# Expert rows loaded as 32-wide squares and transposed by VectorE instead of TensorE

## The chip, the cores and the metric

The kernel runs on one core of a Trainium2 chip. The metric is the device time of one execution in microseconds, the median of several runs.

## The reference, cut to what matters

One layer with attention and a mixture of experts side by side, in fp32. Input `x` has 16 batches of 512 tokens with 128 features; there are 8 experts of hidden width 512, and each token goes to its best two.

```python
xn = layernorm(x)
attn = causal_attention(l2norm(xn @ Wq), l2norm(xn @ Wk), xn @ Wv, scale=8) @ Wo   # 16 heads of 8
probs = softmax(xn @ Wr.T)
top_v, top_i = top_k(probs, 2); top_v = top_v / top_v.sum()
for e in range(8):
    w_e = where(top_i == e, top_v, 0).sum(-1)
    moe += (gelu(xn @ W1[e].T + b1[e]) @ W2[e].T + b2[e]) * w_e
out = x + attn + moe
```

## The kernel before, in words

The first part of the kernel normalises the tokens, routes them and works through the attention of 14 of the 16 batches. Along the way GpSimd sends each normalised token, with its routing data, into a table `slots` in DRAM, sorted by expert: 128 indirect DMAs (`send`). A row of `slots` has 132 floats: 128 features and then the token's place, its first expert, its gate and the difference to the second gate.

The expert stage (`experts`) follows. It takes `slots` in 71 blocks of 256 rows, where a block belongs to one expert. For block i it does the following.

- `fetch(i)` runs on SyncE's queue. It reads the block's expert from `bexp_i`, then issues the loads: the block's rows `xg` (L783), the expert's two weight matrices `w1` (L786) and `w2` (L787), each 256 KB, and the output bias `bb` (L790). The weights go into six buffers that held the transposed tokens `xnT` before, so the profile calls them xnT.
- `turn_rows(i)` makes `xgT`, features on the partitions and 256 tokens along the row: two TensorE transposes into PSUM (L796), a VectorE copy (L798), and three small VectorE instructions for the targets and gates (L801, L807, L811).
- `hidden(i)` multiplies by `w1` (L817), and ScalarE applies gelu (L820) into `gT`.
- `mix(i)` multiplies by `w2` into the one PSUM bank `av` (L828). VectorE adds the bias (L833) and multiplies by the gate (L836), and GpSimd scatters the rows of `y` into the table `results` (the L502 helper).

The order on TensorE, SyncE, VectorE and ScalarE is written out by hand and kept. In step i of the loop stand `hidden(i)`, `turn_rows(i + 1)`, `mix(i - 1)` and at its end `fetch(i + 5)`. The first five fetches come ahead of the loop, and the first of all waits until the last `send` has landed. Each of SyncE's DMAs also waits until the DMA eight places ahead of it on that queue has landed, because eight semaphores go round.

After the blocks come the attention of the last two batches, the loads of `results` (`bring`), the sums into `x` (L908) and the stores.

Of the kernel before, what the change touches and what calls it, by code (L numbers as in the profile page):

```python
# [10 lines left out]
F32 = mybir.dt.float32  # L11
I32 = mybir.dt.int32
AF = mybir.ActivationFunctionType
ALU = mybir.AluOpType
# [10 lines left out]
def attention_moe_kernel(  # L25
# [19 lines left out]
    nc = tc.nc  # L45
    B, S, D = x.shape
    E = wrT.shape[1]
    M = w1T.shape[2]
    P = 128
# [4 lines left out]
    TB = 32  # L54
# [10 lines left out]
    BT = 2 * P  # L65
# [4 lines left out]
    ROW = D + 4  # L70
# [33 lines left out]
    slots = dram.tile([SLOTS, ROW], F32, name="slots")  # L104
# [3 lines left out]
    ident = const.tile([P, P], F32, name="ident")  # L108
# [43 lines left out]
    bexp = keep.tile([P, NB], F32, name="bexp")  # L152
# [18 lines left out]
    def misc(name):  # L171
        return ps_m.tile([P, 512], F32, tag="misc", name=name)
# [49 lines left out]
    def scales(b0, b1, root):  # L222

        cols = slice(b0 * NC, b1 * NC)
        n = (b1 - b0) * NC
        have = {}

        even, odd = st[:, cols, 1], st[:, cols, 4]

        def variance():  # L230
            dif = have["dif"] = sm.tile([P, n], F32, tag="dif", name=f"dif{b0}")
            var = have["var"] = sm.tile([P, n], F32, tag="var", name=f"var{b0}")
            nc.vector.tensor_sub(dif, even, odd)
            nc.vector.tensor_mul(var, dif, dif)
            nc.vector.scalar_tensor_tensor(
                var, var, D / 4.0, st[:, cols, 2], ALU.mult, ALU.add
            )
            nc.vector.tensor_add(var, var, st[:, cols, 5])
            nc.vector.tensor_scalar(var, var, 1.0 / D, LN_EPS, ALU.mult, ALU.add)
            if root:  # L240
                nc.scalar.activation(var, var, AF.Sqrt)

        def first():
            guess(rstd[:, cols], have["var"])
            newton(rstd[:, cols], have["var"], have["dif"], 1)

        def second():
            newton(rstd[:, cols], have["var"], have["dif"], 2)

        def shifts():  # L250
            if root:
                nc.vector.reciprocal(rstd[:, cols], have["var"])
            dif = have["dif"]
            nc.vector.tensor_add(dif, even, odd)
            nc.vector.scalar_tensor_tensor(
                shift[:, cols], dif, -0.5, rstd[:, cols], ALU.mult, ALU.mult
            )

        return [variance, shifts] if root else [variance, first, second, shifts]
# [273 lines left out]
    for r in range(0, NG, 2):  # L533
# [5 lines left out]
        n = len(stages) - PAIR  # L539
# [234 lines left out]
    ep, late = {}, []  # L774

    def fetch(i):
        e = nc.sync.value_load(bexp_i[0:1, i : i + 1], min_val=0, max_val=E - 1)
        xg = ep["w_p"].tile([P, 2, ROW], F32, tag="xg", name=f"xg{i}")

        both = xnT2[i % AHEAD]  # L780
        w1, w2 = both[:, 0], both[:, 1].rearrange("p (m d) -> p m d", d=D)
        bb = ep["w_p"].tile([P, D], F32, tag="bb", name=f"bb{i}")
        nc.sync.dma_start(  # L783
            xg, slots[i * BT : (i + 1) * BT].rearrange("(c p) w -> p c w", p=P)
        )
        nc.sync.dma_start(w1, w1T[:, bass.ds(e, 1)].rearrange("p a m -> p (a m)"))  # L786
        nc.sync.dma_start(  # L787
            both[:, 1], w2T[:, bass.ds(e, 1)].rearrange("p a m d -> p (a m d)")
        )
        nc.sync.dma_start(bb, b2[bass.ds(e, 1)].to_broadcast([P, D]))  # L790
        return dict(xg=xg, w1=w1, w2=w2, bb=bb)

    def turn_rows(i, s):
        pt = misc(f"xgt{i}")
        for c in range(2):
            nc.tensor.transpose(pt[:, ts(c, P)], s["xg"][:, c, :D], ident)  # L796
        s["xgT"] = ep["g_p"].tile([P, BT], F32, tag="xgT", name=f"xgT{i}")
        nc.vector.tensor_copy(s["xgT"], pt[:, :BT])  # L798

        s["to"] = ep["y_p"].tile([P, 2], I32, tag="to", name=f"to{i}")  # L800
        nc.vector.scalar_tensor_tensor(  # L801
            s["to"], s["xg"][:, :, D + 1], bexp[:, i : i + 1], s["xg"][:, :, D],
            ALU.not_equal, ALU.add,
        )

        s["gate"] = ep["y_p"].tile([P, 2], F32, tag="gate", name=f"gate{i}")
        nc.vector.scalar_tensor_tensor(  # L807
            s["gate"], s["xg"][:, :, D + 1], bexp[:, i : i + 1], s["xg"][:, :, D + 3],
            ALU.not_equal, ALU.mult,
        )  # L810
        nc.vector.tensor_add(s["gate"], s["gate"], s["xg"][:, :, D + 2])  # L811

    def hidden(i, s):
        half = ps_sim.tile([P, 2, S], F32, tag="sim", name=f"ph{i}")
# [39 lines left out]
    def first_blocks():  # L854
        for name, bufs in (("w_p", AHEAD), ("g_p", 2), ("y_p", 6)):
            ep[name] = ctx.enter_context(tc.tile_pool(name=name, bufs=bufs))
        for i in range(AHEAD - 1):
            got.append(fetch(i))
        turn_rows(0, got[0])

    def experts():
        for i in range(NB):
            hidden(i, got[i])
            if i == NB - 1:
                scores(FIRST, 0)
                pending.append((FIRST, 0))
            else:
                turn_rows(i + 1, got[i + 1])
            if i < LAG:
                weigh(*pending.pop(0))  # L870
            else:
                mix(i - 1, got[i - 1])
            if i == LAG - 1:
                for n in range(LAG - 1):
                    mix(n, got[n])
            if i % 5 == 4 and i // 5 <= PER:

                for step in plan.pop(PER * FIRST + i // 5, []):
                    step()
            n = i + AHEAD - 1  # L880
            if n < NB:
                got.append(fetch(n))
        mix(NB - 1, got[NB - 1])
        late[:0] = [(PER * FIRST + 6, n) for n in range(FIRST)]
        bring(0)
        bring(1)
# [53 lines left out]
    first = 0  # L940
    for to, base, step, per_partition in (
# [3 lines left out]
        n = to.shape[1]  # L945
# [92 lines left out]
    variance, first, second, shifts = scales(8, B, False)  # L1038
# [73 lines left out]
    t = PER * B  # L1112
# [47 lines left out]
```

## Time and profile before

| | |
|---|---|
| median of 3 runs | 772.0 us (771.88 to 772.14) |
| profiled execution | 773.95 us, span 772.2 us, mean granted clock 0.986 |
| busy: matmul, weight load | 731.1 us (95%), 450.4 us (58%) |
| busy: VectorE, ScalarE, GpSimd | 516.6 (67%), 464.8 (60%), 485.9 us (63%) |
| x transposes on TensorE (L796) | 142, median 273 ns each, first at 432.7, last at 698.3 us |
| copies out of PSUM (L798) | 71, mean 424 ns |
| loads of xg | 71 of 132 KB, first issued at 428.2, last at 683.2 us |

Times in the trace are counted from the start of the span. Busy times are those of one profiled execution. A group's row gives the busy time and the mean of one instruction, then the idle time of the engine just ahead of it and what ended it. The queue that issues DMAs (SPq) is not counted as busy; its issues stand in the timeline only.

### The profile page before, as it was taken

To read this page: it belongs to the slowest core of one execution; us is meant where nothing else is said; L and a number is where in the kernel's file an instruction comes from. 1 tells how busy PE (TensorE), PEld (TensorE's weight loads), DVE (VectorE), ACT (ScalarE), POOL (GpSimd) and SP (SyncE) were. 2 spreads that over 40 slices of the span, in tenths; PEclk is the share of its full clock that TensorE was granted. 3 is DMA by queue.
4 is the path that set the end of the run, shared out by engine and by line. 5 is a ranking of instruction groups with operands and counts; after the bars stand their busy time and mean duration, and the time that the engine had idled before them with its cause. 6 is when DMAs were issued, how large, how long until landed. Compare 5 with 4: busy or idle time off the path is not lost.

```text
span 772.2 us, 17655 instructions
## 1 busy us (share of the span) xinstructions
PE 731.1 (95%) x6478; PEld 450.4 (58%) x6478; DVE 516.6 (67%) x1128; ACT 464.8 (60%) x703; POOL 485.9 (63%) x576
## 2 busy tenths in 40 slices
PE   6899999989999999999999899999999999998994
PEld 2344444334334444444444499989999999996441
DVE  6876678798987887887788445455554445442584
ACT  3767676567777778777878544433444444446771
POOL 4658444388898888888888255554555455556441
PEclk9999999999999999999999999999999999999996
DMA  9940000001101111110110698877777787850596
GB/s 264 326 149 2 1 2 1 1 20 32 33 29 37 37 34 33 36 37 29 38 37 32 194 280 229 229 223 210 235 222 226 222 233 224 233 167 6 187 283 183
DMA packets 91829, 96.48 MB, mean 125 GB/s; under 512 B 10956, under 2 KB 69455, under 8 KB 91744
## 3 DMA queue, kind: packets, MB, share of 16 engines
q1 hardware_dynamic: 82240, 78.01, 35.4%
q0 software_dynamic: 8640, 17.06, 6.5%
q8 instruction: 52, 0.85, 0.4%
q10 hardware_dynamic: 864, 0.28, 0.2%
q14 instruction: 33, 0.27, 0.1%
HBM read 64.34 MB, written 31.88 MB: 125 GB/s over the span
## 4 chain that ended last, share of the span: by engine, by line
PE 80%; DVE 14%; DMA 2%; ACT 1%; issue 1%; POOL 1%; DVEq 0%; POOLq 0%
PE sim L665 17%; PE av L708 17%; PE av L828 16%; PE ph L817 16%; PE proj L561 5%; DMA yt<-results 2%; DVE x L908 2%; PE xgt L796 2%; PE po L752 2%; DVE mid L720 1%; PE qt L619 1%; PE kt L626 1%; DVE st L206 1%; PE idle L959 1%; DVE kT L634 1%
## 5 line engine op out<-in xcount | busy, mean ns | idle before, releaser
L675 ACT ACTIVATE ex<-sim 128x1024 f32<-128x1024 f32 x320 | 310.0, 1022 | 105.4 <-PE sim L665 100.7
L502 POOL DMA_INDIRECT results<-y,to x142 | 139.0, 979 | 138.5 <-DVE y L836 111.8
L820 ACT ACTIVATE gT<-ph,bias 128x256 f32<-128x256 f32 x284 | 111.4, 475 | 158.4 <-PE ph L817 154.0
L665 PE MATMUL sim<-qT,kT 32*128 32x512 f32 (+3 forms) x2048 | 190.1, 463 | 0.7 <-ACT ex L675 0.7
L708 PE MATMUL av<-ex,vaug 128*12 128x512 f32 (+3 forms) x2048 | 171.5, 442 | 16.1 <-DVE mid L720 10.0
L502 POOL TENSOR_SCALAR_AFFINE_SELECT ex<-ex 128x512 f32<-128x512 f32 (+1 forms) x144 | 115.2, 808 | 84.3 <-ACT ex L675 82.6
L502 POOL DMA_INDIRECT slots<-rows,pos x128 | 140.7, 1099 | 28.8 <-issue 25.8
L665 PEld LDWEIGHTS sim<-qT,kT 32*128 32x128 f32 x2048 | 95.7, 185 | 77.8 <-issue 34.0
L828 PE MATMUL av<-xnT,gT 128*128 128x128 f32 x1136 | 138.7, 275 | 1.4 <-ACT gT L820 0.9
L817 PE MATMUL ph<-xgT,xnT 128*128 128x256 f32 x568 | 134.7, 380 | 1.5 <-DVE xgT L798 1.5
L828 PEld LDWEIGHTS av<-xnT,gT 128*128 128x128 f32 x1136 | 132.4, 192 | 2.6 <-issue 1.5
L708 PEld LDWEIGHTS av<-ex,vaug 128*12 128x12 f32 x2048 | 43.0, 92 | 129.3 <-issue 85.5
L817 PEld LDWEIGHTS ph<-xgT,xnT 128*128 128x128 f32 x568 | 102.5, 190 | 13.4 <-DVE xgT L798 1.9
L798 DVE COPY xgT<-xgt 128x256 f32<-128x256 f32 x71 | 30.1, 424 | 68.9 <-PE xgt L796 68.7
L833 DVE TENSOR_TENSOR y<-av,bb 128x256 f32<-128x256 f32 x71 | 30.1, 425 | 67.2 <-PE av L828 67.2
L720 DVE STREAM_TRANSPOSE mid<-av 128x512 f32<-128x512 f32 x64 | 45.5, 711 | 40.6 <-PE av L708 40.4
L561 PE MATMUL proj<-wall,xnT 128*128 128x384 f32 x128 | 58.3, 542 | 5.4 <-DVE xnT L278 2.9
L502 POOL TENSOR_TENSOR qkn<-qkv 128x256 f32<-128x256 f32 x64 | 54.9, 867 | 9.9 <-ACT qkv L564 9.5
L686 DVE TENSOR_TENSOR ex<-ex,causal 128x1024 f32<-128x1024 f32 x40 | 52.0, 1300 | 3.4 <-ACT ex L675 3.4
L634 DVE TENSOR_SCALAR kT<-kr,hmask 128x512 f32<-128x512 f32 x64 | 40.5, 635 | 0.6
L564 ACT COPY qkv<-proj 128x384 f32<-128x384 f32 x64 | 30.9, 482 | 14.1 <-PE proj L561 13.9
L561 PEld LDWEIGHTS proj<-wall,xnT 128*128 128x128 f32 x128 | 19.5, 190 | 32.6 <-issue 16.3
(144 smaller groups left out, 584.8 us busy)
## 6 DMA issues: line engine op xcount, KB each, us to landing
xnT<-in_w1T_dram SPq DMA_DIRECT2D x71, 256.0 KB, 3.5
xnT<-in_w2T_dram SPq DMA_DIRECT2D x71, 256.0 KB
slots<-fill SPq DMA_DIRECT2D x48, 198.0 KB, 5.1
xg<-slots SPq DMA_DIRECT2D x71, 132.0 KB
yt<-results SPq DMA_DIRECT2D x16, 512.0 KB, 5.1
bb<-in_b_dram SPq DMA_DIRECT2D x71, 64.0 KB
x<-in_x_dram SPq DMA_DIRECT2D x16, 256.0 KB, 4.7
out_dram<-x SPq DMA_DIRECT2D x16, 256.0 KB, 5.5
```

What stands on the lines that cost most here:

```text
L502: ins = op(*args, **kw)
L561: nc.tensor.matmul(pp[:, :NQKV], xnT[b][:, ts(c, P)], wall, start=True, stop=True)
L564: nc.scalar.copy(s["qkv"][:, c], pp[:, :NQKV])
L634: nc.vector.tensor_scalar_mul(s["kT"][:, r], s["kr"], hmask[:, r : r + 1])
L665: nc.tensor.matmul(halves[g // 2][:, g % 2, col : col + (NC - j) * P], s["kT"][group, r, ts(j, P)], s["qT"][group, j * P :], start=True, s ...
L675: nc.scalar.activation(ex[:, 2 * h : 2 * h + 2], half, AF.Exp, scale=SCALE)
L686: nc.vector.tensor_mul(diag, diag, causal.unsqueeze(1).unsqueeze(1).to_broadcast([P, NG, many, P]),)
L708: nc.tensor.matmul(av[32 * g : 32 * g + VW, j * P :], s["vaug"][:, j, NG * g + r], s[m][:, g, col : col + (NC - j) * P], start=(j == 0), s ...
L720: nc.vector.transpose(s["mid"][:, r], av)
L817: nc.tensor.matmul(ph[:, m], s["w1"][:, ts(m, P)], s["xgT"], start=True, stop=True)
L820: nc.scalar.activation(s["gT"][:, m], ph[:, m], AF.Gelu, bias=bias1[:, i, m : m + 1])
L828: nc.tensor.matmul(py[:, c], s["gT"][:, m, ts(c, P)], s["w2"][:, m], start=(m == 0), stop=(m == NM - 1),)
```

## The change

In `fetch`, the one load of a block's rows is replaced by five loads. Four of them bring the features: load f takes features 32f to 32f + 31 of all 256 rows, and puts them on partitions 32f to 32f + 31 of a tile `z`. Partition 32f + p then holds, side by side, the 32-float pieces of the rows p, p + 32, p + 64 and so on, so each piece is 128 bytes long. The fifth load brings the last four floats of each row, the routing data, into a tile `tell`, in pieces of 16 bytes. In `turn_rows`, one VectorE transpose, which turns each 32 by 32 square in place, makes `xgT` from `z`; the TensorE transposes and the copy are left out. The gate instructions read `tell` where they read `xg`.

```diff
-        xg = ep["w_p"].tile([P, 2, ROW], F32, tag="xg", name=f"xg{i}")
+        z = ep["w_p"].tile([P, BT], F32, tag="z", name=f"z{i}")
+        tell = ep["w_p"].tile([P, 2, ROW - D], F32, tag="tell", name=f"tell{i}")
...
-        nc.sync.dma_start(
-            xg, slots[i * BT : (i + 1) * BT].rearrange("(c p) w -> p c w", p=P)
-        )
+        mine = slots[i * BT : (i + 1) * BT]
+        for f in range(D // TB):
+            nc.sync.dma_start(
+                z[ts(f, TB)].rearrange("p (t f) -> p t f", f=TB),
+                mine[:, ts(f, TB)].rearrange("(t p) f -> p t f", p=TB),
+            )
+        nc.sync.dma_start(tell, mine[:, D:].rearrange("(c p) w -> p c w", p=P))
...
     def turn_rows(i, s):
-        pt = misc(f"xgt{i}")
-        for c in range(2):
-            nc.tensor.transpose(pt[:, ts(c, P)], s["xg"][:, c, :D], ident)
         s["xgT"] = ep["g_p"].tile([P, BT], F32, tag="xgT", name=f"xgT{i}")
-        nc.vector.tensor_copy(s["xgT"], pt[:, :BT])
+        nc.vector.transpose(s["xgT"], s["z"])
+        token, first, gate, more = (s["tell"][:, :, n] for n in range(4))
```

More of the change, by code (lines that the diff above doesn't have):

```diff
@@ L790, in fetch @@
         nc.sync.dma_start(bb, b2[bass.ds(e, 1)].to_broadcast([P, D]))
-        return dict(xg=xg, w1=w1, w2=w2, bb=bb)
+        return dict(z=z, tell=tell, w1=w1, w2=w2, bb=bb)
     def turn_rows(i, s):
-        pt = misc(f"xgt{i}")
-        for c in range(2):
-            nc.tensor.transpose(pt[:, ts(c, P)], s["xg"][:, c, :D], ident)
         s["xgT"] = ep["g_p"].tile([P, BT], F32, tag="xgT", name=f"xgT{i}")
-        nc.vector.tensor_copy(s["xgT"], pt[:, :BT])
+        nc.vector.transpose(s["xgT"], s["z"])
+        token, first, gate, more = (s["tell"][:, :, n] for n in range(4))
         s["to"] = ep["y_p"].tile([P, 2], I32, tag="to", name=f"to{i}")
         nc.vector.scalar_tensor_tensor(
-            s["to"], s["xg"][:, :, D + 1], bexp[:, i : i + 1], s["xg"][:, :, D],
-            ALU.not_equal, ALU.add,
+            s["to"], first, bexp[:, i : i + 1], token, ALU.not_equal, ALU.add
         )
@@ L807, in turn_rows @@
         nc.vector.scalar_tensor_tensor(
-            s["gate"], s["xg"][:, :, D + 1], bexp[:, i : i + 1], s["xg"][:, :, D + 3],
-            ALU.not_equal, ALU.mult,
+            s["gate"], first, bexp[:, i : i + 1], more, ALU.not_equal, ALU.mult
         )
-        nc.vector.tensor_add(s["gate"], s["gate"], s["xg"][:, :, D + 2])
+        nc.vector.tensor_add(s["gate"], s["gate"], gate)
     def hidden(i, s):
```

## The prediction

> **What bounds the kernel now.** I read the busy table first, then the windows of the expert stage, its chain of waits, the timeline of SyncE's queue, and last the DMA rows. In the expert stage TensorE never rests:
>
> ```profile
> 520.00:560.00 40.00, 40.00 (x281) 37.11 (x280) 19.88 (x70) 16.30 (x42) 20.39 (x21) 1.00 0.76 222
> 560.00:600.00 40.00, 40.00 (x282) 37.31 (x281) 19.98 (x67) 16.66 (x43) 21.12 (x21) 1.00 0.79 229
> 600.00:640.00 40.00, 40.00 (x283) 37.32 (x282) 19.29 (x67) 17.02 (x44) 21.32 (x22) 1.00 0.76 222
> ```
>
> The columns are matmul, weight load, VectorE, ScalarE and GpSimd busy time, the granted clock, the DMA share and GB/s. TensorE fills every window at full clock, VectorE half of it, and the 16 DMA engines are already 0.77 busy. The chain over 520 to 640 us, and three rows of the page:
>
> ```profile
> by line: PE av L828 47.2%; PE ph L817 45.6%; PE xgt L796 5.9%; PE po L752 0.7%; PE qt L619 0.4%; PE kt L626 0.4%
> ...
> L798 DVE COPY xgT<-xgt 128x256 f32<-128x256 f32 x71 | 30.1, 424 | 68.9 <-PE xgt L796 68.7
> L720 DVE STREAM_TRANSPOSE mid<-av 128x512 f32<-128x512 f32 x64 | 45.5, 711 | 40.6 <-PE av L708 40.4
> xg<-slots SPq DMA_DIRECT2D x71, 132.0 KB
> ```
>
> So the chain is matmuls alone, and the transposes to be removed are 5.9% of it. A block takes 3.73 us: the first x transposes stand at 501.20, 504.93 and 508.66. What decides the case is a queue that these rows don't count as busy. SyncE's timeline before the blocks are PE-bound, and then inside the bound part:
>
> ```profile
> 431.03 0.38 SPq L783 DMA_DIRECT2D xg<-slots  x1
> 431.61 0.33 SPq L786 DMA_DIRECT2D xnT<-in_w1T_dram  x1
> 432.12 0.33 SPq L787 DMA_DIRECT2D xnT<-in_w2T_dram  x1
> 432.63 0.33 SPq L790 DMA_DIRECT2D bb<-in_b_dram  x1
> 433.61 0.38 SPq L783 DMA_DIRECT2D xg<-slots  x1
> ...
> 504.93 0.38 SPq L783 DMA_DIRECT2D xg<-slots  x1
> 505.50 0.33 SPq L786 DMA_DIRECT2D xnT<-in_w1T_dram  x1
> 507.13 0.33 SPq L787 DMA_DIRECT2D xnT<-in_w2T_dram  x1
> 507.70 0.33 SPq L790 DMA_DIRECT2D bb<-in_b_dram  x1
> 508.67 0.38 SPq L783 DMA_DIRECT2D xg<-slots  x1
> ```
>
> First number: start; second: the queue's time for the issue. Running free, SyncE needs 2.6 us for one block's four DMAs; in the bound part it needs 3.73 because the w2 load waits for a free buffer (1.63 us after w1 instead of 0.5). The waits say so too:
>
> ```profile
> SPq L787 <- PE av L828: 29.8, 29, 2.1
> ```
>
> That is 1.0 us of waiting per block (29.8 us over 29 blocks). SyncE has about one microsecond per block to spare, no more.
>
> **The change, part by part, per block.**
>
> *Removed on TensorE:* two transposes and their weight loads. They show 0.38 us as matmul time, but overlap the next weight loads; the chain's share is the price: 5.9% of 120 us over 32 blocks is 0.22 us. TensorE's own period becomes 3.73 - 0.22 = 3.51 us.
>
> *VectorE:* a 128x256 copy out of PSUM (424 ns) becomes a 128x256 transpose in SBUF. No such transpose is in the trace; the nearest rows are the 128x512 ones, 711 ns from PSUM and 704 ns from SBUF (oT). It lies between half of the latter, 0.35, and the whole, 0.70; copies run 0.69 us at 512 and 0.42 at 256, so I take 0.43. VectorE is half idle, so this costs nothing; its cover is the idle half, and with that gone it would cost 0.01 (0.28 at the upper end). The three small gate instructions keep their shape. The transpose now waits for four z loads directly, and behind it on VectorE stand the tell readers and the previous block's y addition, which frees the av bank for the next w2 matmuls. Those stand behind the next block's w1 matmuls, and w1 is issued after z and tell, so this wait ends no later than one that exists anyway: no extra.
>
> *SyncE:* one load of xg becomes four loads of z and one of tell; w1, w2 and bb follow behind. Eight issues instead of four. Without any hold-up the old four cost: starts at 428.21, 431.03, 433.61, 436.24, 438.95, 441.65, 444.40, 447.14, that is 18.93 us over 7 blocks, 2.70 us, including the read of the expert's number (0.98 us from bb to the next xg). The tell load takes xg's place: 256 pieces as before, and w1 0.58 us behind it. Each z load is 256 pieces too, like xg, which took 0.38 us; z needs no register work, so the gap to the next is what the trace shows between two such issues late in the kernel (735.06 + 0.36, next at 735.47): 0.05. I take 0.43 per z load. Lower end 0.37 (the 128-piece fill at 0.32 plus the gap), upper end 0.58 (xg's step with register work). Period of SyncE: 2.70 + 4 x 0.43 = 4.42 us, between 4.18 and 5.02. That is above TensorE's 3.51 and above today's 3.73: the spare microsecond is used up, and the queue becomes the bound.
>
> Here the trace and the Trainium skill differ. "DMA: Bandwidth & Descriptors", section "Issuing engines are not separate DMA queues", holds that the sequencer's time to start a DMA is usually small beside the DMA. By that rule the four added issues are free, the period is 3.51 and the kernel gains some 14 us. By the row above an issue with its gap costs 0.43 us while the 16 engines move its 32 KB in 0.24 us (next part); I go by the row.
>
> *The 16 DMA engines:* today 0.77 x 3.73 = 2.87 us per block. xg's 256 pieces of 528 B go; 1024 pieces of 128 B, 256 of 16 B and 64 more completion writes come. No 128-byte load stands in this stage, but the b1 load near the start is one:
>
> ```profile
> q10 hardware_dynamic: 416, 0.19, 38.2%
> ...
> q10 hardware_dynamic: 160, 0.02, 7.0%
> ```
>
> These are ScalarE's queue at 4 to 6 us (nearly all 512-byte pieces) and at 6 to 8 us (128 of 128 B, 32 completions): 0.382 x 16 x 2 us / 416 = 29 ns, and 0.070 x 32 us / 160 = 14 ns. So 15 ns for 128 B and about 10 for the smallest. Sum: 2.87 - 256 x 30/16 (0.48) + 1024 x 15/16 (0.96) + 256 x 10/16 (0.16) + 0.04 = 3.55 us per block, below 4.42: hidden. If that cover were gone, it would still only meet TensorE's own period. The same page's "Specifications" asks for at least 512 B per piece and has smaller ones read, modified and written. If a small piece were to cost what a 512-byte one does, the sum is 2.39 + 1.86 + 0.46 + 0.12 = 4.83 us, and the DMA engines pass SyncE. The row says half of that price for a 128-byte piece; it was measured beside x loads, not on rows 528 B apart, so the rule stays in the range.
>
> *DMA waits in the queue:* every SyncE DMA waits for the one eight before it to have landed; that was two blocks ago, now it is one. w1 lands 2.8 to 5.5 us after issue, median 3.5. With 4.42 us between the same loads of two blocks the median passes; a few late ones may add 0.1 to the period.
>
> *Elsewhere:* GpSimd's scatters keep their number and are released by the same y. TensorE will idle 0.9 us per block; the clock is granted at 1.00 in the first 50 us too, where it idles 10, so I count no loss.
>
> **The sum.** Block 0's first load starts at 428.21 as before (it waits for the last scatter of rows). Block 70's starts at 428.21 + 70 x 4.42 = 737.6; its w1 is issued 4 x 0.43 + 0.58 = 2.3 later and lands 3.5 after: 743.4. Before, block 70's first-layer matmuls started at 700.2, five blocks of prefetch behind the last load; that lead is eaten. Everything after (last blocks, last attention, combining) hangs on it in the same order: +43 us. Against the profiled execution (773.95 us, span 772.2) that is 817; it stood 1.95 above the median of the runs, 772.0, so I forecast 815.
>
> **The rivals.**
>
> *DMA engines bound (15%).* Small pieces at the 512-byte price, or the late landings above becoming the rule: 4.83 us per block, 428.2 + 70 x 4.83 + 5.8 - 700.2 = +72, so about 844. For it: the stage stands at 0.77 already, and single packets will queue behind 2 KB ones. Against: the 14 ns row.
>
> *TensorE stays the bound, faster (3%).* If a z issue, writing only 32 partitions, costs SyncE much less, its period falls below the old one. Setting 428.2 + 70 x (2.70 + 4s) + 4s + 4.1 = 700.2 gives s = 0.28 us: below that the change gains, down to 772 - 66 blocks x 0.22 = 758. Against: the shortest DMA issue anywhere in the trace is the fill's 0.319, before any gap.
>
> *The change doesn't do what it says (1%).* The instruction order shows no transposes on TensorE and four z loads a block, so only a hidden order change could do that; about 772.
>
> **How the numbers follow.** SyncE bound: 0.81, its own range 2.70 + 4 x 0.37 to 2.70 + 4 x 0.50, 4.18 to 4.70 us: 798 to 835. With the DMA case the range is 798 to 848, leaving out issue costs near 0.58 and the faster tail. About 0.2% is what this measurement can tell from no change. Faster 0.03, within 0.2% 0.01, slower 0.96.
>
> **What would show it.** Right: SyncE's timeline in the stage has z issues 0.43 us apart without waits, L787's wait on the av matmuls gone, TensorE busy near 80% in the windows, DMA share near 0.8, and matmuls waiting for w1 landings. Wrong: a DMA share at 1.0 or above with SyncE waiting for its own earlier DMAs (DMA bound), or a period of 3.5 us with the wait of the w2 load still there (TensorE bound). A clock below 1.00 in the stage would mean that the idle time costs more than itself.

## The result and the profile after

The changed kernel takes 850.7 us (median of 4 runs, 847.7 to 855.5) against 772.1 us: a ratio of 1.102, 95% interval 1.096 to 1.108. That is slower, as forecast, and for the forecast mechanism. But it is 79 us slower where 43 were forecast, and it lies just above the range's end of 848. The profiled execution took 848.73 us, with a span of 847.0.

The same windows of the expert stage:

```profile
520.00:560.00 40.00, 31.79 (x209) 28.66 (x207) 18.39 (x61) 13.34 (x35) 15.97 (x17) 1.00 0.70 175
560.00:600.00 40.00, 30.00 (x193) 27.07 (x193) 15.74 (x53) 12.56 (x32) 16.12 (x17) 1.00 0.71 179
600.00:640.00 40.00, 31.13 (x199) 28.09 (x200) 15.20 (x50) 12.56 (x32) 16.09 (x17) 1.00 0.72 173
```

TensorE, full before, is now 75 to 79% busy at full clock. No other engine took over: VectorE, ScalarE and GpSimd all fell, and so did the DMA share, from 0.77 to 0.71. When every busy column falls, the bound is likely something that these columns leave out. The page's chain of work that ended last, and the same chain over 520 to 720 us, name it:

```profile
PE 44%; SPq 20%; DVE 14%; DMA 12%; issue 6%; POOL 3%; ACT 1%; DVEq 0%; POOLq 0%
...
by line: SPq L788 23.0%; DMA z<-slots 14.9%; DMA xnT<-in_w1T_dram 10.2%; issue 9.8%; PE ph L820 8.9%; SPq L777 6.9%; SPq L794 4.3%; SPq L797 4.1%; SPq L792 3.6%; SPq L793 3.3%; DVE xgT L802 3.2%; PE av L831 2.7%; DMA tell<-slots 1.3%; DVE y
```

SPq is SyncE's queue of issues. It was not among the chain's entries before. One block on it, without a hold-up, and the start of the next (start, time of the issues together, number of them at the end):

```profile
544.84 1.81 SPq L788 DMA_DIRECT2D z<-slots  x4
546.70 0.45 SPq L792 DMA_DIRECT2D tell<-slots  x1
547.35 0.36 SPq L793 DMA_DIRECT2D xnT<-in_w1T_dram  x1
547.95 0.35 SPq L794 DMA_DIRECT2D xnT<-in_w2T_dram  x1
548.54 0.33 SPq L797 DMA_DIRECT2D bb<-in_b_dram  x1
549.50 1.81 SPq L788 DMA_DIRECT2D z<-slots  x4
```

From z at 544.84 to z at 549.50 a clean block takes 4.66 us. The mean is longer: the register work ahead of w1 runs from 430.6 to 773.4 us over 70 blocks, 4.90 us each. The queue hardly waits for anything. These are its two longest waits over 520 to 640 us:

```profile
SPq L797 <- DVE xgT L802: 3.0, 11, 0.4
SPq L794 <- PE ph L820: 0.7, 3, 0.4
```

The w2 load (L794 here, L787 before) waited 29.8 us for the av matmuls in this window before; now it waits for none of them. No entry is a DMA, so the wait for the DMA eight places ahead, which the prediction feared, costs nothing here. The short waits of bb (L797) for the transpose are places where the chain leaves the queue for a landing of z. The other end of the queue is seen in the row of the new transpose. Its 445 ns are close to the copy's 424, but VectorE now stands idle ahead of it until z lands:

```profile
L802 DVE STREAM_TRANSPOSE xgT<-z 128x256 f32<-128x256 f32 x71 | 31.6, 445 | 186.1 <-DMA z<-slots 186.1
```

### The profile page after: what moved, and what is told of

The parts are those of the page before. It is cut to its first block, busy times and chain, and to the rows that moved or that the text cites. A ratio compares the mean times of both kernels' runs of the same rounds, so it can differ in the third digit from the quotient of the medians.

```text
span 847.0 us, 17732 instructions
## 1 busy us (share of the span) xinstructions
PE 731.1 (86%) x6336; PEld 441.9 (52%) x6336; DVE 518.9 (61%) x1128; ACT 464.8 (55%) x703; POOL 487.5 (58%) x576
## 4 chain that ended last, share of the span: by engine, by line
PE 44%; SPq 20%; DVE 14%; DMA 12%; issue 6%; POOL 3%; ACT 1%; DVEq 0%; POOLq 0%
PE av L708 14%; PE sim L665 14%; SPq L788 10%; DMA z<-slots 5%; PE proj L561 4%; PE ph L820 4%; DMA xnT<-in_w1T_dram 3%; SPq L777 3%; DMA yt<-results 3%; PE av L831 2%; SPq L794 2%; SPq L797 2%; SPq L792 2%; SPq L793 2%; DVE x L911 2%
## 5 line engine op out<-in xcount | busy, mean ns | idle before, releaser
L820 PE MATMUL ph<-xgT,xnT 128*128 128x256 f32 x568 | 139.8, 389 | 77.8 <-DMA xnT<-in_w1T_dram 49.1
L802 DVE STREAM_TRANSPOSE xgT<-z 128x256 f32<-128x256 f32 x71 | 31.6, 445 | 186.1 <-DMA z<-slots 186.1
L831 PEld LDWEIGHTS av<-xnT,gT 128*128 128x128 f32 x1136 | 137.8, 192 | 6.1 <-issue 1.5
```

The lines of the kernel that those rows point to most:

```text
L820: nc.tensor.matmul(ph[:, m], s["w1"][:, ts(m, P)], s["xgT"], start=True, stop=True)
L831: nc.tensor.matmul(py[:, c], s["gT"][:, m, ts(c, P)], s["w2"][:, m], start=(m == 0), stop=(m == NM - 1),)
```

## The experiments

Two theories can make a block 4.9 us long. By the first, the time that SyncE takes for its eight issues is the bound. By the second, it is the 128-byte pieces, in the DMA engines or through late landings. Times below are medians. Chips differ, so ratios are against runs of the kernel before on the same chip; it took 772 us there, except for e5_six to e8_before_merged, where it took 780.6.

**The issues without the pieces, and the pieces without the issues.** Both start from the kernel before and keep TensorE's transposes.

```diff
 # e3_issues
-        nc.sync.dma_start(xg, slots[...].rearrange("(c p) w -> p c w", p=P))
+        for q in range(4):
+            nc.sync.dma_start(xg[ts(q, TB)], mine[ts(q, TB), :, :D])
+        nc.sync.dma_start(tell, mine[:, :, D:])
```

> The kernel before with the features loaded by four DMAs of 32 partitions each in 512-byte pieces (64 to a DMA) and the routing data by a fifth: the issues of the change, without its 128-byte pieces and without its VectorE transpose. If the number of issues is the bound, 815 to 850 us: 849 if such an issue takes the 0.49 us that a z load took, 815 if a quarter of the pieces brings it down to 0.37. If 128-byte pieces are the bound, 772 to 780.

Measured: 845.2 us, ratio 1.091 (1.085 to 1.097). Eight issues without any 128-byte piece bring back 73 of the 79 us. Its queue:

```profile
563.25 1.74 SPq L786 DMA_DIRECT2D xg<-slots  x4
565.03 0.43 SPq L787 DMA_DIRECT2D tell<-slots  x1
565.65 0.36 SPq L788 DMA_DIRECT2D xnT<-in_w1T_dram  x1
566.26 0.35 SPq L789 DMA_DIRECT2D xnT<-in_w2T_dram  x1
566.85 0.33 SPq L792 DMA_DIRECT2D bb<-in_b_dram  x1
567.81 0.33 SPq L786 DMA_DIRECT2D xg<-slots  x1
```

Here a block takes 4.56 us. The four loads have only 64 pieces each, yet take 1.74 us together, against 1.81 for 256 pieces each. So at this size it is the issue that costs, hardly its pieces.

```diff
 # e2_pieces
-        nc.sync.dma_start(xg, slots[...].rearrange("(c p) w -> p c w", p=P))
+        pieces = slots[...].rearrange("(p c) (g v) -> p (c g) v", c=2, v=TB + 1)
+        nc.sync.dma_start(xg.rearrange("p c (g f) -> p (c g) f", f=TB), pieces[:, :, :TB])
+        nc.sync.dma_start(tell, mine[:, :, D:])
```

> The kernel before with the features loaded in 1024 pieces of 128 bytes by a single DMA, and the routing data by a second one: the pieces of the change, without its issues and without its VectorE transpose (each piece starts one float later in its row than it should, so the features are shifted). SyncE then needs 2.7 + 0.65 = 3.35 us a block, under today's 3.73. If issues are the bound, 770 to 776 us, as before. If pieces are the bound, a block takes 4.8 to 4.9 us and the kernel 835 to 850.

Measured: 783.1 us, ratio 1.013 (1.006 to 1.019). The kernel computes on shifted features here, in the same 71 blocks. The pieces theory asked for 835 or more and falls. But 783 is also above the 770 to 776 expected of the issue theory; the queue and the chain over 480 to 680 us show where it comes from:

```profile
562.04 0.52 SPq L786 DMA_DIRECT2D xg<-slots  x1
562.60 0.67 SPq L789 DMA_DIRECT2D tell<-slots  x1
563.46 0.45 SPq L790 DMA_DIRECT2D xnT<-in_w1T_dram  x1
564.16 0.34 SPq L791 DMA_DIRECT2D xnT<-in_w2T_dram  x1
564.74 0.33 SPq L794 DMA_DIRECT2D bb<-in_b_dram  x1
565.71 0.52 SPq L786 DMA_DIRECT2D xg<-slots  x1
...
by line: PE av L832 35.2%; PE ph L821 30.9%; DMA xg<-slots 10.7%; PE xgt L800 5.1%; issue 3.4%; SPq L777 2.3%; SPq L790 2.2%; SPq L789 2.0%; SPq L794 1.5%; SPq L786 1.3%; DVE y L837 1.1%; SPq L791 1.1%; DVE y L840 0.6%; DVE ss L585 0.6%; PE
```

An issue of 1024 pieces takes 0.52 us instead of 0.38, and the two behind it are slowed as well (0.67 and 0.45). This block takes 3.67 us on the queue, so the spare microsecond is gone with five issues already. With hold-ups the blocks take 3.93 us on average (bb runs from 431.2 to 706.1 us over 70 blocks), more than TensorE's 3.73. So the prefetch falls behind, and landings of xg enter the chain.

**One issue less, one issue more.** Both edit the changed kernel.

```diff
 # e4_tell_many, MANY = 8
-        nc.sync.dma_start(tell, mine[:, D:].rearrange("(c p) w -> p c w", p=P))
+        if i % MANY == 0:
+            nc.sync.dma_start(tells[-1][:, :n], slots[i * BT : i * BT + n * P, D:]...)
+        tell = tells[-1][:, 2 * (i % MANY) : 2 * (i % MANY) + 2]
```

> The changed kernel with the routing data of eight blocks loaded by one DMA, so that seven in eight of the tell loads are gone: one issue less on SyncE per block, the same pieces. If SyncE's issue time is the bound, each block gains the 0.6 us that the tell step takes: 70 x 7/8 x 0.6 = 37 us, so 808 to 818 us. If the DMA engines are the bound, nothing is saved: 843 to 850.

Measured: 833.5 us, ratio 1.077 (1.071 to 1.083): a gain of 17 us over the changed kernel, between the two theories. The queue explains both the gain and what is missing from it:

```profile
538.75 0.38 SPq L786 DMA_DIRECT2D tells<-slots  x1
539.17 4.02 SPq L797 DMA_DIRECT2D z<-slots  x4
...
562.66 1.84 SPq L797 DMA_DIRECT2D z<-slots  x4
564.69 0.36 SPq L801 DMA_DIRECT2D xnT<-in_w1T_dram  x1
565.30 0.36 SPq L802 DMA_DIRECT2D xnT<-in_w2T_dram  x1
565.90 0.33 SPq L805 DMA_DIRECT2D bb<-in_b_dram  x1
566.87 1.32 SPq L797 DMA_DIRECT2D z<-slots  x3
```

A block without the shared load takes 4.21 us, 0.45 less than 4.66. But the shared load has 2048 pieces, and the z issues right behind it are slowed. The first and the third of the four that take 4.02 us:

```profile
539.17 1.70 SPq L797 DMA_DIRECT2D z<-slots  x1
541.42 1.28 SPq L797 DMA_DIRECT2D z<-slots  x1
```

The first takes 1.70 us instead of 0.33. Behind all nine shared loads it takes 1.22 to 2.23 us, 1.84 on average. The third is another matter: it lies beside a large packet of an instruction queue, a hold-up that the next section comes to. The shared load costs 1.5 us behind it and its own step of 0.42, once in eight blocks: 0.24 us per block. 0.45 - 0.24 = 0.21, times 70 is an estimate of 15 us, of the 17. Pieces are not free to the queue; they cost when thousands of them stand ahead of the next issue.

```diff
 # e7_one_more
+        nc.sync.dma_start(again, mine[:, D:].rearrange("(c p) w -> p c w", p=P))
```

> The changed kernel with the tell load issued twice, the second into a tile that nothing reads: one issue of 4 KB more per block. If SyncE's issues are the bound, a block takes 0.49 us more and the kernel 70 x 0.49 = 34 us more: 880 to 890. If the DMA engines are the bound, the 256 pieces of 16 bytes add 0.14 us a block, 10 us: 858 to 862. If something else is the bound, 851.

Measured: 895.2 us, ratio 1.149 (1.146 to 1.151). Against the changed kernel's 1.102, that is 0.047 x 772 = 36 us for one 4 KB load per block, where issues were to cost 34 and DMA time 10. So one more issue costs the kernel about its step on the queue. (In its own trace, on the other chip, a block takes 5.50 us on the queue, 0.60 more than the changed kernel's, so hold-ups may have grown too.)

**The same DMAs from another queue.** The changed kernel with z issued by ScalarE.

```diff
 # e1_z_on_act
-            nc.sync.dma_start(z[...], mine[...])
+            nc.scalar.dma_start(z[...], mine[...])
```

> The changed kernel with its four z loads issued from ScalarE's queue instead of SyncE's: the same DMAs, the same pieces, four issues fewer on SyncE. If SyncE's issue time is the bound, its period falls from 4.9 us by 4 x 0.47 to about 3.0, below TensorE's 3.5; ScalarE then has 1.9 us of gelu and 4 x 0.49 us of issues per block, about 3.9, and the kernel takes 765 to 790 us. If the small pieces bind the DMA engines, or the landings of earlier DMAs do, it stays at 840 to 850.

Measured: 801.1 us, ratio 1.034 (1.027 to 1.040). The same bytes in the same pieces lose 50 us less, so neither pieces nor DMA bandwidth were the bound of the changed kernel. It missed the expected 765 to 790: by the waits and the chain over 480 to 680 us, ScalarE's gelu now stands in line behind z issues that wait for earlier DMAs, and landings seem the limit here.

```profile
ACT gT L823 <- DMA z<-slots: 86.8, 33, 3.8
...
by line: DMA z<-slots 76.6%; PE av L831 5.2%; DMA tell<-slots 4.7%; ACT gT L823 4.3%; issue 2.7%; ACTq L788 2.7%; PE ph L820 1.7%; DMA bb<-in_b_dram 1.5%; DVE y L836 0.9%; DVE x L756 0.3%; SPq L777 0.3%; DVE y L839 0.3%; DVE xgT L802 0.2%; 
```

The stage also started late, with its first matmul at 449.1 us instead of the changed kernel's 434.7.

**Relieving the queue, step by step.** `e5_six` loads both weight matrices by one DMA and the routing data of four blocks by one. `e6_six_half_act` also issues every second z from ScalarE. `e8_before_merged` is the control: only the weights merged, in the kernel before.

```diff
-        nc.sync.dma_start(w1, w1T[:, bass.ds(e, 1)]...)
-        nc.sync.dma_start(both[:, 1], w2T[:, bass.ds(e, 1)]...)
+        nc.sync.dma_start(both.rearrange("p a m -> p (a m)"), w12[:, bass.ds(e, 1)]...)
 # e6_six_half_act
-            nc.sync.dma_start(z[...], mine[...])
+            (nc.sync, nc.scalar)[f % 2].dma_start(z[...], mine[...])
```

> The changed kernel with w1 and w2 loaded by one DMA (one array laid out so in DRAM) and the routing data of four blocks by one DMA: 6.25 issues per block on SyncE instead of 8, with the same 128-byte pieces. If SyncE's steps are the bound, a period of 0.38 + 3 x 0.49 for z, 0.65, 0.60 and 0.97 less one z step counted twice, that is 3.6, plus 0.12 for the shared tell load and 0.2 to 0.4 of hold-ups: 3.9 to 4.1, so 780 to 795 us. If pieces or the DMA engines are the bound, 840 or more.

> As e5_six, with every second z load issued from ScalarE: SyncE then needs 2.7 us a block and ScalarE 1.9 + 1.0, so neither is a bound. TensorE's 3.51 us and the DMA engines (0.71 x 4.9 = 3.5 us in the changed kernel, perhaps 0.2 less with the longer weight pieces) are then what is left. If the issue theory holds and TensorE's saving is real, 757 to 770 us, under the kernel before; if the DMA engines take over at 3.5 us and TensorE waits for single late pieces, 772 to 785. If pieces had been the bound all along, over 830.

> The kernel before with w1 and w2 loaded by one DMA, as in e5_six and e6_six_half_act: one issue fewer for SyncE and longer pieces for the DMA engines. TensorE binds the kernel before, so nothing should be gained: 770 to 774 us. If DMA late landings cost the kernel before something that its chain doesn't show, up to 5 us less.

Measured, each against the kernel before: e5_six 1.027 (1.024 to 1.029), 800.3 us; e6_six_half_act 0.997 (0.996 to 0.999), 778.4 us; e8_before_merged 0.999 (0.997 to 1.000), 778.7 us. On this slower chip e5_six's ratio answers to 793 us of 772, inside its 780 to 795. Merging the weights alone shows no clear gain. e6_six_half_act answers to 770 us of 772, the upper edge of the 757 to 770 that it was to take with TensorE's saving. Its chain in the stage is matmuls again, but its first block came late: ScalarE's first z issues stood still until 441.9 us.

```profile
441.94 7.20 ACTq L796 DMA_DIRECT2D z<-slots  x7
```

**A version that beats both.** As e6_six_half_act, but the first five blocks' z loads stay on SyncE.

```diff
 # e9_half_act_later
+        second = nc.sync if i < AHEAD - 1 else nc.scalar
-            (nc.sync, nc.scalar)[f % 2].dma_start(...)
+            (nc.sync, second)[f % 2].dma_start(...)
```

> As e6_six_half_act, but the first five blocks' z loads all come from SyncE and only later blocks use ScalarE for every second one. In e6_six_half_act the blocks ran at 3.63 us each against 3.82 in the kernel before (13 us over 70 blocks), and the first block began 14 us late because ScalarE's first z issue came only at 441.9 us. If that late start is what ate the gain, this kernel is 1.0% to 1.8% faster than the kernel before. If the saving per block is lost again to late DMA landings, it is within 0.3% of it.

Measured: 763.6 us against 772.4, ratio 0.988 (0.986 to 0.991), inside the expected gain of 1.0 to 1.8%. Its windows and the chain over 600 to 640 us:

```profile
520.00:560.00 40.00, 39.76 (x271) 36.94 (x270) 19.98 (x73) 17.27 (x44) 20.88 (x23) 1.00 0.96 243
560.00:600.00 40.00, 40.00 (x278) 37.73 (x277) 19.56 (x69) 17.94 (x46) 22.71 (x24) 1.00 0.97 241
600.00:640.00 40.00, 40.00 (x279) 37.73 (x278) 19.20 (x69) 17.83 (x47) 22.32 (x23) 1.00 0.94 237
...
by line: PE av L839 51.9%; PE ph L828 47.5%; PE kt L625 1.1%
...
606.70 1.78 PE av L839 x16
610.21 1.78 PE av L839 x16
613.72 1.78 PE av L839 x16
```

TensorE is full again and the blocks shown follow each other at 3.51 us, the saving that the edit was able to give. Over the whole stage less is kept: from block 0's first-layer matmuls to block 70's it is 3.66 us per block, against 3.80 before. The DMA share of 0.94 to 0.97 says how little is left before the DMA engines would be the next bound.

## Why the prediction was right or wrong

- *The bound.* Right. SyncE's issues took TensorE's place; e3_issues, e7_one_more and e1_z_on_act each show it, and the DMA share went to 0.71 instead of the rival's 1.0. That the rival's 844 us lies nearer to the measured 851 than the forecast does is chance: its mechanism did not occur.
- *The sum.* Wrong, by the period of a block: 4.42 us forecast, 4.90 measured. The difference of 0.48 times 70 blocks is 34 us, and 817 + 34 = 851 answers to the profiled 848.7. Half of it is the price of the issues, half a term that the sum did not have. The prediction's own upper end of the period, 5.02 us, held 4.90, but its range of times left that tail out.
- *The z issue.* This step was mis-sized: "I take 0.43 per z load", from an issue that stood first in its line. In the changed kernel z loads start at 544.84, 545.22, 545.71 and 546.20, and tell at 546.70: the first step is 0.38, the others 0.49. An issue right behind another takes 0.45 us, not 0.33. The trace of before had the warning. In the pair used for the gap the second issue took 0.69 us against 0.36, and three early fills in a row, the DMA that the prediction takes its shortest issue of 0.319 us from, show the step of 0.49 to 0.50 us:

```profile
15.20 0.46 SPq L971 DMA_DIRECT2D slots<-fill  x1
15.70 0.45 SPq L971 DMA_DIRECT2D slots<-fill  x1
16.20 0.45 SPq L971 DMA_DIRECT2D slots<-fill  x1
```

  Four steps make 1.86 instead of 1.72, tell to w1 0.65 instead of 0.58, the rest 2.15 instead of 2.12: 4.66, and 17 us over 70 blocks.
- *Hold-ups.* Missing from the sum: 0.24 us per block between the clean 4.66 and the mean 4.90, the other 17 us. The prediction thought of 0.1 for late landings, and left it out of the sum; this is something else. Single issues take 0.8 to 1.6 us. The fourteen longest of the stage exceed their usual time by 11 us together, and each lies beside one large packet of the instruction queue q8. One of them, with the DMA queues of 551 to 556 us:

```profile
552.00 1.42 SPq L793 DMA_DIRECT2D xnT<-in_w1T_dram  x1
...
q8 instruction: 1, 0.02, 1.6%
```

  The kernel before has such hold-ups too (its w1 issue at 447.72 us took 0.92), and its wait for a free buffer could absorb them. In the changed kernel the queue has no such wait left. That the instruction fetch causes the stall is argued from the coincidence; no run here changed the fetches, so the cause stays open.
- *TensorE's saving.* Right: 0.22 us per block was forecast, and its own period of 3.51 us appears to the digit in the clean blocks of e9_half_act_later. In the changed kernel it is all spent waiting.
- *VectorE's transpose.* Right: 0.43 us taken, 445 ns measured, and e3_issues loses as much without it.
- *The DMA engines.* Right within what was shown: 0.71 x 4.90 = 3.48 us of work per block, against 3.55 in the sum. The rule of the Trainium skill on pieces under 512 bytes ("DMA: Bandwidth & Descriptors", section "Specifications"), kept in the range as a rival, did not come true as the bound: e3_issues, with features in 512-byte pieces, is hardly faster. Small pieces still cost something by way of the queue and of their landings, and e2_pieces loses 1.3% with them.
- *The rule on issues.* The Trainium skill (same page, section "Issuing engines are not separate DMA queues") has the time to start a DMA as usually small beside the DMA. Its sum gave a gain of some 14 us. e7_one_more decides against it here: about 36 us for a load of 4 KB per block.

## What to carry to other kernels

Before splitting one DMA into several, count the issues per period on the queue that sends them and price each by its step within a run of issues, not by a lone one: here 0.49 us and not 0.43. Then leave room for hold-ups. A queue isn't in the busy table. Its spare time is the time it waits for buffers, here 1.0 us per block; what an edit adds beyond that lengthens the kernel in full, hold-ups included. When a saving on the bounding engine doesn't show, look first for the wait or queue that took its place: with 4.25 of the eight issues per block left on SyncE (two z loads moved to ScalarE, the others merged) and a clean start, the same edit was 1.2% faster instead of 10% slower.

## What the runs showed of the hardware that was not expected

- The time of an issue depends little on its pieces up to a few hundred (four issues: 1.74 us at 64 pieces each, 1.81 at 256). The cost of more pieces falls mostly on the issue behind: an issue of 2048 pieces took 0.38 us itself, and the next 1.84 on average instead of 0.33.
- The granted clock fell in one of two runs in which TensorE idles in much the same way: in e7_one_more's windows from 480 to 680 us it was 0.91 to 0.96 with TensorE 72 to 80% busy, while in the changed kernel's windows it stayed at 1.00. Both were bound by the queue; whether the lower clock cost anything, no run here separates.
